# Score rounds in pairs in the middle steps, a reordered start, and shift and scale read back from DRAM

## The chip, the cores and the metric

The kernel runs on one core of a Trainium2 chip. The metric is the device time in microseconds (us) of one execution; the median of several runs is compared. A core has five engines that run side by side and meet at semaphores: PE (TensorE, matrix products), DVE (VectorE), ACT (ScalarE), POOL (GpSimd) and SP (SyncE, which here only issues transfers). PE writes to PSUM, which has eight banks; ACT and DVE read results from there.

## The reference

The input x is 8 sequences (B) of 256 tokens with 256 channels. Four blocks follow one another, each added to x. Cut to what matters:

```
x = x + attention_and_swiglu(x, cond)         # L0: conditioned norm, 16 heads of 16, softmax; then a gated MLP (1024)
x = x + modulated_attention(x, mask, cond)    # L1: 16 heads; out is normalised, then out * (1 + scale) + shift
x = x + quaternion_rotation(x)                # L2: reduces to a fixed 4x4 mixing of channel quarters
x = x + experts(x, cond)                      # L3: top 2 of 8 experts, three matrix products each

# L1's shift and scale, per sequence:
mod = silu(cond) @ Wc.T + bc                  # 8 x 512
shift, sc = split(mod);  xn = xn * rms_scale * (1 + sc) + shift
```

## The kernel before

**Order of work.** The program runs the sequences as a pipeline. A list `queue` holds the attention work of both layers in rounds: first layer "a0" of sequences 0, 1, 2, then in turn "a1" of sequence i and "a0" of sequence i+3. One call of `block()` (L1690) takes the next round: it computes scores for 8 heads (`c`) and half of the keys (`kc`), and if a pair of score rounds is complete, the values of that earlier pair. So each (sequence, layer) has four rounds, (c, kc) = (0,0), (0,1), (1,0), (1,1); values come behind the scores of the rounds with kc = 0, of the `c` before.

**A score round** (`Attention.scores`, L983) is eight matmul instructions on four groups of 32 rows of the array, into one PSUM tile of four banks (`ps_s`, one buffer), and one exponential over it on ACT (L990). **A values round** (L993) is 32 matmul instructions on four groups of 32 columns, into one bank (`ps_o`). All else on PE (projections, gates, transposes) shares three banks in turn (`ps_m`, through `bank()`), so a new tile waits until the third tile before it has been read.

**Steps.** `run(what, pieces, gaps, beside, starts)` (L1705) writes the order: for each letter "b" in `what` a round, then pieces of other work until the gap given for it is spent, `starts` before the pieces and `beside` after them. What a round's values complete (`then`: `after_first` with py, y; or `after_second` with py, o1) is done after three pieces. The middle steps are i = 2 to 6, each a `run("bbbbbbbb", others(i - 1), ...)` at L1901. `others` gives the pieces: gates pg, ph in four pairs with tanh (ACT), sg and hT (DVE), the product pd, then x2, its transpose pt_x, and the projections pk, pq, pv of the next rounds. `starts` and `beside` hold: `last` (the router of an earlier group, in steps 4 and 6, with four squarings on ACT at first), `n1` (norm of the sequence after next: squarings, then the divisor on DVE and two small transfers, then scaling), `n2` (the norm before the gates: squarings on ACT, divisor on DVE, two scalings on ACT, L900), `r1` and `rotated` (rotation on DVE).

In the whole program PE's instructions stand in the order of the text (`manual_schedule`), in the start DVE, ACT and POOL too, and DVE and ACT again from the middle steps on. SP's transfers go out in order, and each waits for its own data at the head of the queue.

**The start.** `first_norm(b)` yields three times: squarings, the divisor (`rsqrt`, eleven small DVE operations), the scaling. `first(b)` yields after the transposes (pt_n), pk, pq, pv. `prepare_condition` (L690) makes silu of the condition and `keyseen` from the mask; `prepare_router` (L748) prepares router constants; `set_up_condition` (L712) computes `mod` (8 x 512) on PE and writes it to DRAM as `mod_rows`, from where each sequence's row is later broadcast.

**Shift and scale on partitions.** `set_up_rotation` (L804) needs the same numbers the other way round, as `mc` (128 partitions x 4 x 8): it computes them a second time, in eight matmul instructions `pmc` (four products, L833) and two DVE operations. `scaled` reads `mc`, then come `phall`, `pshift`, `each`, and `pshg` (L862), one part after another as `second_step` (L1854) calls them.

Of the kernel before, what the change touches and what calls it, by code (L numbers as in the profile page):

```python
# [16 lines left out]
P = 128  # L17
# [17 lines left out]
WROW = B3O + D  # L35

SMALL = dict(condT=B, qrT=4, sgT=1, affb=4 * KC, rms=KC, wg=KC * E, ggw=E, wgb=E, ggb=E,
             wg4=4 * E, rms4=4, bcc=2 * KC, rsc=KC)

SL = 256  # L40

# [452 lines left out]
def block_kernel(ctx: ExitStack, tc: tile.TileContext, a: dict, out: bass.AP):  # L494
# [217 lines left out]
    def set_up_condition():  # L712

        pm = bank("pmod", (B, 2 * D))
        nc.tensor.matmul(pm, silu_c, wcT, start=True, stop=True)
        mod = wt("oT", [B, 2 * D], "mod_all")
        nc.vector.tensor_tensor(mod, pm, bc_b, ALU.add)
        nc.vector.scalar_tensor_tensor(mod[:, D:], mod[:, D:], 1.0, rs_b, ALU.add, ALU.mult)
        nc.gpsimd.dma_start(out=mod_rows, in_=mod)
        yield 0.4  # L720

    def set_up_slots():
# [81 lines left out]
    def set_up_rotation():  # L804
        prepare_rotation()

        nc.vector.tensor_tensor(
            wg4s, part["wg4"].rearrange("p (j e) -> p j e", e=E),
            part["rms4"].unsqueeze(2).to_broadcast([P, 4, E]), ALU.mult,
        )  # L810
        for h in range(2):
            r = slice(h * C, (h + 1) * C)
            nc.vector.tensor_copy(rmine[r], rotg[r].rearrange("p j (k h) -> p k h j", h=2)[:, :, h, :])
        turned = work.tile([P, KC, 4, E], F32, tag="raw", bufs=2, name="turned")
        nc.vector.tensor_tensor(
            turned, rmine.unsqueeze(3).to_broadcast([P, KC, 4, E]),
            wg4s.unsqueeze(1).to_broadcast([P, KC, 4, E]), ALU.mult,
        )
        nc.vector.tensor_reduce(gall, turned.rearrange("p k j e -> p k e j"), AX.X, ALU.add)
        nc.vector.tensor_copy(wv1[:, :, D:], gall)  # L820

        nc.sync.dma_start(out=coef_row, in_=rotg[0:C].rearrange("c j i -> c (j i)"))
        rows_in = wt("x4", [P, C, 4, 4], "coef_in", 1)
        nc.sync.dma_start(
            out=rows_in.rearrange("p c j i -> p (c j i)"),
            in_=coef_row.rearrange("c w -> (c w)").partition_broadcast(P),
        )
        yield
        nc.gpsimd.tensor_copy(coef, rows_in.rearrange("p c j i -> p i j c"))

        pm = bank("pmc", (P, 2 * KC, B))
        for k in range(2 * KC):
            nc.tensor.matmul(pm[:, k, :], wcT[:, k * P : (k + 1) * P], silu_c, start=True, stop=True)  # L833
        nc.vector.tensor_tensor(mc, pm, part["bcc"].unsqueeze(2).to_broadcast([P, 2 * KC, B]), ALU.add)
        nc.vector.scalar_tensor_tensor(
            mc[:, KC:], mc[:, KC:], 1.0, part["rsc"].unsqueeze(2).to_broadcast([P, KC, B]), ALU.add, ALU.mult
        )
        scaled = wt("mod", [P, KC, B, E], "scaled")
        nc.vector.tensor_tensor(
            scaled, mc[:, KC:].unsqueeze(3).to_broadcast([P, KC, B, E]),  # L840
            gall.unsqueeze(2).to_broadcast([P, KC, B, E]), ALU.mult,
        )
        yield
        ph = bank("phall", (P, KC, B * E))
        for c in range(KC):
            for k in range(KC):
                nc.tensor.matmul(
                    ph[:, c, :], wo1n[:, k, c * P : (c + 1) * P], scaled[:, k].rearrange("p b e -> p (b e)"),
                    start=k == 0, stop=k == KC - 1,
                )  # L850
        nc.vector.tensor_copy(hall.rearrange("p k b e -> p k (b e)"), ph)
        ps = bank("pshift", (B, E))
        for k in range(KC):
            nc.tensor.matmul(ps, mc[:, k, :], gall[:, k, :], start=k == 0, stop=k == KC - 1)
        each = work.tile([B, B, E], F32, tag="r_each", bufs=1, name="each")
        nc.vector.tensor_tensor(
            each, ps.unsqueeze(1).to_broadcast([B, B, E]),
            ident[0:B, 0:B].unsqueeze(2).to_broadcast([B, B, E]), ALU.mult,
        )
        yield  # L860
        pb = bank("pshg", (P, B * E))
        nc.tensor.matmul(pb, ones[0:B, :], each.rearrange("p b e -> p (b e)"), start=True, stop=True)  # L862
        nc.vector.tensor_copy(shg.rearrange("p b e -> p (b e)"), pb)
        yield
# [5 lines left out]
    def bank(name, shape=(P, 2, S)):  # L870
        return ps_m.tile(list(shape), F32, tag="m", name=name)
# [165 lines left out]
    def do(parts):  # L1037
        for _ in parts:
            pass
# [650 lines left out]
    def block():  # L1690
        layer, b, c, kc = queue.pop(0)
        second = layer == "a1"
        if (c, kc) == (0, 0):
            live[layer, b] = Attention(
                state[b].pop(f"qkv{int(second)}"), f"{layer}_{b}", (2 * b + second) * KC
            )
        live[layer, b].scores(c, kc)
        then = values()
        if second and (c, kc) == (KC - 1, NQ - 1):
            nc.vector.tensor_copy(wo1[:, :, D:], hall[:, :, b, :])  # L1700
        if kc == NQ - 1:
            pending.append((layer, b, c))
        return then

    def run(what, pieces, us=0.0, beside={}, rest=True, owed=None, hold=False, soon=3, late_=(), starts={}):  # L1705

        spent, due, held = 0.0, 0.0, None
        for t, kind in enumerate(what):
            then = block() if kind == "b" else values() if kind == "v" else None
            do_deferred()
            for g in starts.get(t, ()):
                next(g, None)
            if held:
                held()  # L1720
                spent += 1.9
            held = None
            then, owed = then or owed, None
            if t in late_:
                held, then = then, None
            gap = us if isinstance(us, float) else us[t]
            due = max(due + gap, spent + min(gap, 3.0))
            n = 0
            while spent < due or (then and n < soon):
                w = next(pieces, "end")  # L1730
                if w == "break":
                    due = spent
                if w in ("break", "end"):
                    break
                spent += 1.9 if w is None else w
                n += 1
                if then and n == soon:
                    then()
                    spent += 1.9
                    then = None  # L1740
            if then and hold:
                return then
            if then:
                then()
                spent += 1.9
            for g in beside.get(t, ()):
                next(g, None)
        if rest:
            for _ in pieces:
                pass  # L1750

    def chain(*gens):
        for g in gens:
            yield from g
# [52 lines left out]
    with tc.manual_schedule(engines=by_text):  # L1807
# [10 lines left out]
        next(g0)  # L1818
        keep_busy(2)
        scales()  # L1820
        n1 = first_norm(1)
        next(n1)
        next(n1)
        next(g0)
        next(g0)
        do(n1)
        do(g0)
        blank = set_up_slots()
        prepare_condition()
        cond_g = prepare_router()  # L1830
        finish_slots(*blank)
        def third(b):

# [8 lines left out]


        operands = first(1)
        run("b", chain(take(1, operands), set_up_condition(), set_up_router(cond_g)), 9.0, rest=False)
        run("b", take(1, operands), 9.0, {0: [once(prepare_quaternions)]}, rest=False)
        n1 = first_norm(2)
        run("b", iter(()), 0.0, {0: [n1]})
        run("b", operands, 9.0, {0: [at_once(n1)]}, rest=False)
# [4 lines left out]
        def second_step():  # L1854
            rotation = set_up_rotation()
            next(rotation)
            yield
            n1 = first_turned(3)
            next(n1)
            yield  # L1860
            n2 = in_parts(1, "n2")
            next(n1)
            next(n2)
            next(rotation)
            yield
            do(n1)
            next(n2)
            next(rotation)
            set_up_ones()
            yield  # L1870
            do(n2)
            yield from rotation

        set_up = second_step()
        gaps = [1.9, 5.0, 7.2, 7.2, 7.2, 7.2]
        run("bbbbbb", chain(operands, others(0)), gaps, {n: [set_up] for n in range(1, 6)}, soon=2)
    by_text = {mybir.EngineType.DVE, mybir.EngineType.Activation}
    text_order = ctx.enter_context(ExitStack())
    text_order.enter_context(tc.manual_schedule(engines=by_text))
# [1 line left out]
    for i in range(2, B - 1):  # L1881
# [14 lines left out]
        if i == B - 2:  # L1896
# [1 line left out]
            early = table("early", (NG - 2) * NTG, EARLY, ALU.is_ge)  # L1898
            beside[4].insert(0, early)
            beside[7].append(early)  # L1900
        run("bbbbbbbb", others(i - 1), gaps, beside, late_=() if i + 2 < B else (4,), starts=starts)  # L1901


    pieces = others(B - 2)
# [206 lines left out]
```

## Time and profile before

| | |
|---|---|
| median of 8 runs | 703.54 us (703.05 to 706.36) |
| profiled execution: its own time | 706.39 us |
| its span, first to last instruction | 704.6 us |
| granted TensorE clock, mean | 0.997 |
| PE busy | 691.1 us (98%) |
| DVE, ACT, POOL busy | 366.1 (52%), 255.4 (36%), 180.3 (26%) |

Stages of the span, from first score round to first score round:

| stage | us | PE busy | DVE busy | ACT busy |
|---|---|---|---|---|
| up to the first scores | 0 to 18.60 | 17.10 | 7.33 | 5.55 |
| start, sequences 0 to 2 | 18.60 to 95.30 | 75.59 | 41.91 | 36.77 |
| step 2 | 95.30 to 148.48 | 53.16 | 30.24 | 23.74 |
| step 3 | 148.48 to 201.65 | 53.15 | 32.03 | 23.94 |
| step 4 | 201.65 to 255.87 | 53.78 | 38.64 | 25.92 |
| step 5 | 255.87 to 309.03 | 53.14 | 31.87 | 23.93 |
| step 6 | 309.03 to 358.49 | 48.60 | 36.83 | 24.52 |
| end of the attention | 358.49 to 441.0 | 81.49 | 54.48 | 32.85 |
| experts | 441.0 to 704.6 | 255.13 | 92.73 | 58.16 |

All times are those of one profiled execution, counted from its first instruction. A timeline line gives the start, the length, the engine, the line of the program, the operation, what it writes and reads, and in brackets how long the engine was idle before it and what ended that. Matmul instructions overlap, so the distance from one start to the next says more than the length. "PEld" is PE's loading of weights beside the products.

### The profile page before, as it was taken

Reading aid. Unit: us, or ns where it says so; the run is one execution under the profiler, and the core shown is the slowest. Engines: PE = TensorE matmul, PEld = TensorE weight load, DVE = VectorE, ACT = ScalarE, POOL = GpSimd, SP = SyncE. Lnnn points to the kernel's source line nnn. Section 1 sums busy time; section 2 is a strip of 40 time slices with the busy share of each in tenths; the row PEclk is TensorE's granted clock in tenths of the full one; section 3 lists DMA queues with packets and bytes.
Section 4 is the critical chain, followed back from the end, with each engine's and each line's share of the span. In section 5 each row is a group of like instructions: output and inputs, shape, how many; then the busy total and the mean of one; then the engine's idle time right before and its main releaser. Section 6 shows DMA issues by size and latency. Waiting matters only on the chain.

```text
span 704.6 us, 11187 instructions
## 1 busy us (share of the span) xinstructions
PE 691.1 (98%) x4258; PEld 534.0 (76%) x4258; DVE 366.1 (52%) x1165; ACT 255.4 (36%) x411; POOL 180.3 (26%) x223
## 2 busy tenths in 40 slices
PE   9999999999999999999999999999999999999995
PEld 8557777667766766766666786688888998999894
DVE  3664436576478476477575686688321222222221
ACT  3663234344354345355434236322221222222120
POOL 5511401001000141000230016324374432342213
PEclk9999999999999999999999999999999999999998
DMA  9411101002022000020000050837585866576712
GB/s 304 146 32 45 39 1 38 1 16 39 5 71 39 0 18 8 1 75 1 2 16 1 16 203 10 308 127 218 145 289 157 236 240 193 170 266 191 253 26 29
DMA packets 28878, 70.01 MB, mean 99 GB/s; under 512 B 9032, under 2 KB 22224, under 8 KB 26384
## 3 DMA queue, kind: packets, MB, share of 16 engines
q1 hardware_dynamic: 20032, 57.70, 24.8%
q0 software_dynamic: 8496, 11.32, 7.4%
q8 instruction: 35, 0.57, 0.3%
q14 instruction: 27, 0.22, 0.1%
q10 hardware_dynamic: 288, 0.18, 0.1%
HBM read 59.67 MB, written 9.53 MB: 98 GB/s over the span
## 4 chain that ended last, share of the span: by engine, by line
PE 92%; DVE 5%; ACT 2%; issue 1%; POOL 0%; POOLq 0%; DVEq 0%; ACTq 0%
PE ph_a_rest L1528 10%; PE s_a L988 9%; PE pd L1141 8%; PE pg L1128 8%; PE ph_a_p L1528 7%; PE ph L1128 7%; PE o_a L1001 7%; PE ph_s_sure L1528 6%; PE pq_a L932 3%; PE pe_a_rest L1558 3%; PE pk_a L932 3%; PE pe_a_p L1558 3%; PE pv_a L954 2%; PE py L1024 2%; PE pe_s_sure L1558 2%; PE py L1174 2%
## 5 line engine op out<-in xcount | busy, mean ns | idle before, releaser
L990 ACT ACTIVATE pe_a<-s_a 128x2048 f32<-128x2048 f32 x64 | 120.1, 1876 | 100.3 <-PE s_a L988 100.2
L988 PE MATMUL s_a<-qz_a,kT_a 32*128 32x512 f32 x512 | 73.0, 639 | 2.4 <-DVE xg L1159 0.9
L1001 PE MATMUL o_a<-pe_a,va 128*32 128x256 f32 x1024 | 61.9, 382 | 0.0
L1128 PE MATMUL pg<-xT_n,gate_wT 128*128 128x256 f32 x256 | 61.8, 384 | 0.0
L1128 PE MATMUL ph<-xT_n,hid_wT 128*128 128x256 f32 x256 | 61.6, 383 | 0.0
L1001 PEld LDWEIGHTS o_a<-pe_a,va 128*32 128x32 f32 x1024 | 30.0, 109 | 39.9 <-issue 23.4
L1141 PE MATMUL pd<-out_wT,hT 128*128 128x256 f32 x256 | 59.7, 384 | 0.4 <-DVE hT L1136 0.4
L1141 PEld LDWEIGHTS pd<-out_wT,hT 128*128 128x128 f32 x256 | 47.4, 190 | 13.7 <-issue 4.0
L1128 PEld LDWEIGHTS ph<-xT_n,hid_wT 128*128 128x128 f32 x256 | 47.7, 190 | 13.3 <-DVE rq_v_n L619 2.3
L1128 PEld LDWEIGHTS pg<-xT_n,gate_wT 128*128 128x128 f32 x256 | 47.6, 190 | 12.0 <-issue 3.6
L1010 DVE STREAM_TRANSPOSE tu_a<-o_a 128x512 f32<-128x512 f32 x32 | 22.8, 712 | 52.3 <-PE o_a L1001 52.3
L1528 PE MATMUL ph_a_rest<-h_a_rest,w_a_rest 128*128 128x256 f32 x224 | 49.6, 379 | 0.0
L1528 PEld LDWEIGHTS ph_a_rest<-h_a_rest,w_a_rest 128*128 128x128 f32 x224 | 42.0, 190 | 5.4
L1101 POOL TENSOR_TENSOR xy<-y,x 128x512 f32<-128x512 f32 x8 | 10.2, 1270 | 139.2 <-DVE rq_v_r L619 55.0
L1539 DVE TENSOR_SCALAR h_a_rest<-ph_a_rest,w_a_rest 128x256 f32<-128x256 f32 x28 | 13.6, 484 | 57.3 <-PE ph_a_rest L1528 56.3
L1316 POOL DMA_INDIRECT slots<-rec,posi x32 | 31.8, 994 | 22.6 <-issue 7.3
L1134 DVE SCALAR_TENSOR_TENSOR sg<-th,pg 128x512 f32<-128x512 f32 x32 | 21.9, 685 | 28.3 <-ACT th L1132 28.3
L988 PEld LDWEIGHTS s_a<-qz_a,kT_a 32*128 32x128 f32 x512 | 20.0, 182 | 21.5 <-issue 13.4
L1528 PE MATMUL ph_a_p<-h_a_p,w_a_p 128*128 128x192 f32 (+2 forms) x224 | 36.0, 319 | 0.0
L1132 ACT ACTIVATE th<-pg 128x512 f32<-128x512 f32 x32 | 19.0, 594 | 46.4 <-PE pg L1128 46.4
L1537 ACT ACTIVATE h_a_rest<-ph_a_rest,w_a_rest 128x256 f32<-128x256 f32 x28 | 13.3, 473 | 60.7 <-DVE h_a_rest L1539 60.7
L1528 PEld LDWEIGHTS ph_a_p<-h_a_p,w_a_p 128*128 128x128 f32 x224 | 34.9, 191 | 0.1
(351 smaller groups left out, 1185.8 us busy)
## 6 DMA issues: line engine op xcount, KB each, us to landing
w_a_rest<-in_experts SPq DMA_DIRECT2D x7, 2180.0 KB, 9.5
w_a_p<-in_experts SPq DMA_DIRECT2D x7, 2180.0 KB, 9.1
w_s_sure<-in_experts SPq DMA_DIRECT2D x4, 2180.0 KB, 10.2
w_s_early<-in_experts SPq DMA_DIRECT2D x1, 2180.0 KB, 8.7
mod<-mod_rows SPq DMA_DIRECT2D x8, 256.0 KB, 3.3
tokens<-x SPq DMA_DIRECT2D x4, 512.0 KB, 3.8
out<-x SPq DMA_DIRECT2D x4, 512.0 KB, 4.9
x<-in_x SPq DMA_DIRECT2D x7, 256.0 KB, 2.8
```

Of the source, the lines that this page charges most:

```text
L932: nc.tensor.matmul(pp[:, c, :], w[:, k, c * P : (c + 1) * P], xT[:, k, :], start=k == 0, stop=k == KC - 1)
L988: nc.tensor.matmul(sc[:, j], kT[r, c, kc * P : (kc + 1) * P], qz[r, c], start=True, stop=True)
L990: nc.scalar.activation(pe, sc, AF.Exp)
L1001: nc.tensor.matmul(o[32 * i : 32 * i + 32, qd, :], va[:, kc, 8 * c + 4 * qd + i].rearrange("p a d -> p (a d)"), pe[:, 2 * qd + i // 2, i % ...
L1010: nc.vector.transpose(turned.rearrange("p q j a d -> p (q j a d)"), o.rearrange("p q s -> p (q s)"))
L1128: nc.tensor.matmul(ps[:, j, :], w[:, k, o : o + P], yT[:, k, :], start=k == 0, stop=k == KC - 1)
L1132: nc.scalar.activation(th, pg, AF.Tanh, scale=0.5)
L1134: nc.vector.scalar_tensor_tensor(sg, th, 1.0, pg, ALU.add, ALU.mult)
L1141: nc.tensor.matmul(pd[:, t, :], hT[:, c, t * P : (t + 1) * P], out_w[:, c, :], start=c == 0, stop=c == HID // P - 1)
L1316: sc = nc.gpsimd.indirect_dma_start(out=slots, out_offset=bass.IndirectOffsetOnAxis(ap=posi[:, t : t + 1], axis=0), in_=rec[:, t, :], in_o ...
L1528: nc.tensor.matmul(ph[:, c - c0, 0:many], w[:, o : o + P], src[:, k, 0:many], start=k == 0, stop=k == n_in - 1,)
L1558: nc.tensor.matmul(pos[q][0:p, q, :], h2[:, k, q * p : (q + 1) * p], w[:, o : o + D], start=k == 0, stop=k == MC - 1,)
```

## The change

Four edits.

- In the middle steps two score rounds stand next to each other: with `pairs=True` the even letters call `block()` twice, the odd ones none. The gaps, the pieces and what stands beside them stay.
- In the start the condition and router constants come ahead of the norm of sequence 1; that norm's divisor comes behind the first queries, its scaling behind the first score round; pt_n and pk of sequence 1 both come behind the second round.
- `mc` is read from `mod_rows` in DRAM, in four transfers on SP's queue with a transposing access pattern, in place of the four products and two DVE operations. Its two columns of constants leave the small input.
- The last part of the rotation constants (`pshg`) comes at the head of the sixth round of the second stage's run, ahead of the last part of n2.

```diff
-             wg4=4 * E, rms4=4, bcc=2 * KC, rsc=KC)
+             wg4=4 * E, rms4=4)
...
         nc.gpsimd.dma_start(out=mod_rows, in_=mod)
+        for j in range(2 * KC):
+            nc.sync.dma_start(out=mc[:, j, :], in_=mod_rows[:, j * P : (j + 1) * P].rearrange("b p -> p b"))
...
         nc.gpsimd.tensor_copy(coef, rows_in.rearrange("p c j i -> p i j c"))
-        pm = bank("pmc", (P, 2 * KC, B))
-        for k in range(2 * KC):
-            nc.tensor.matmul(pm[:, k, :], wcT[:, k * P : (k + 1) * P], silu_c, start=True, stop=True)
-        nc.vector.tensor_tensor(mc, pm, part["bcc"]..., ALU.add)
-        nc.vector.scalar_tensor_tensor(mc[:, KC:], mc[:, KC:], 1.0, part["rsc"]..., ALU.add, ALU.mult)
         scaled = wt("mod", [P, KC, B, E], "scaled")
...
-            then = block() if kind == "b" else values() if kind == "v" else None
+            then = None
+            if pairs:
+                if t % 2 == 0:
+                    then = block()
+                    block()
+            else:
+                then = block() if kind == "b" else values() if kind == "v" else None
...
         scales()
+        prepare_condition()
+        cond_g = prepare_router()
         n1 = first_norm(1)
         next(n1)
-        next(n1)
         next(g0)
         next(g0)
-        do(n1)
+        next(n1)
         do(g0)
         blank = set_up_slots()
-        prepare_condition()
-        cond_g = prepare_router()
         finish_slots(*blank)
...
-        run("b", chain(take(1, operands), set_up_condition(), set_up_router(cond_g)), 9.0, rest=False)
-        run("b", take(1, operands), 9.0, {0: [once(prepare_quaternions)]}, rest=False)
+        run("b", chain(set_up_condition(), set_up_router(cond_g)), 9.0, {0: [at_once(n1)]}, rest=False)
+        run("b", take(2, operands), 9.0, {0: [once(prepare_quaternions)]}, rest=False)
...
             set_up_ones()
             yield
+            next(rotation)
+            yield
             do(n2)
-            yield from rotation
...
-        run("bbbbbb", chain(operands, others(0)), gaps, {n: [set_up] for n in range(1, 6)}, soon=2)
+        run("bbbbbb", chain(operands, others(0)), gaps, {n: [set_up] for n in range(1, 6)}, soon=2, starts={5: [set_up]})
...
-        run("bbbbbbbb", others(i - 1), gaps, beside, late_=() if i + 2 < B else (4,), starts=starts)
+        run("bbbbbbbb", others(i - 1), gaps, beside, late_=() if i + 2 < B else (4,), starts=starts, pairs=True)
```

More of the change, by code (lines that the diff above doesn't have):

```diff
@@ L829, in set_up_rotation @@
         nc.gpsimd.tensor_copy(coef, rows_in.rearrange("p c j i -> p i j c"))
-        pm = bank("pmc", (P, 2 * KC, B))
-        for k in range(2 * KC):
-            nc.tensor.matmul(pm[:, k, :], wcT[:, k * P : (k + 1) * P], silu_c, start=True, stop=True)
[L834 to L837, printed above, removed]
         scaled = wt("mod", [P, KC, B, E], "scaled")
@@ L1703, in block, with run @@
         return then
-    def run(what, pieces, us=0.0, beside={}, rest=True, owed=None, hold=False, soon=3, late_=(), starts={}):
+    def run(what, pieces, us=0.0, beside={}, rest=True, owed=None, hold=False, soon=3, late_=(), starts={}, pairs=False):
         spent, due, held = 0.0, 0.0, None
         for t, kind in enumerate(what):
-            then = block() if kind == "b" else values() if kind == "v" else None
+            then = None
[5 more added lines that the diff above has]
+                then = block() if kind == "b" else values() if kind == "v" else None
             do_deferred()
@@ L2083 @@
         rms4=np.tile(v["L3_cond_rms_w"].reshape(4, C).T, (2, 1)),
-        bcc=chunks(v["L1_cond_bc"]),
-        rsc=chunks(v["L1_cond_rms_scale"]),
     )
```

## The prediction

> **What bounds the kernel now.** I read the page's chain first (PE carries 92% of it), then PE's waits, then PE's timeline through one middle step, then ACT and DVE beside the places where the change moves work. In PE's waits (us in total, times, longest) nothing is left to win: six waits in 704.6 us, 4.5 us together.
>
> ```profile
> ...
> PE s_a L988 <- DVE xg L1159: 0.9, 1, 0.9
> ...
> PE pd L1141 <- DVE hT L1136: 0.4, 1, 0.4
> PE s_a L988 <- ACT pe_a L990: 0.2, 1, 0.2
> ```
>
> PE's timeline in step i = 3 (start us, us, what): a score round (s_a), a values round (o_a), and the "other" pieces pg, ph, pd between them.
>
> ```profile
> 153.24 1.89 PE L1128 MATMUL ph<-xT_n,hid_wT 128*128 128x256 f32 x8
> 154.97 1.89 PE L1128 MATMUL pg<-xT_n,gate_wT 128*128 128x256 f32 x8
> 156.70 1.89 PE L1024 MATMUL py<-L_WoT_turned,oT_a 128*128 128x256 f32 x8
> 158.52 1.14 PE L988 MATMUL s_a<-qz_a,kT_a 32*128 32x512 f32 x8
> 159.59 1.99 PE L1128 MATMUL ph<-xT_n,hid_wT 128*128 128x256 f32 x8
> 161.42 1.89 PE L1128 MATMUL pg<-xT_n,gate_wT 128*128 128x256 f32 x8
> ...
> 166.04 1.93 PE L1001 MATMUL o_a<-pe_a,va 128*32 128x256 f32 x32
> 167.90 1.99 PE L1128 MATMUL pg<-xT_n,gate_wT 128*128 128x256 f32 x8
> ```
>
> From start to start a piece of eight matmuls takes 1.73 (153.24 to 154.97), 1.82 when a score round follows (156.70 to 158.52) and 1.83 when one went before (159.59 to 161.42). A score round takes 1.07 (158.52 to 159.59), values after scores 1.86 (166.04 to 167.90). So each visit from the full array to these rounds, which split it into four groups, costs 0.09 + 0.10 = 0.19 beside its own work. The exponential of a score round (128x2048 on ACT) takes 1.88, and the scores have one buffer: the next round may start only after it.
>
> **The pairs themselves: +0.4 (0 to +1.4).** A pair before is scores, values, pieces, scores: 1.07 + 1.86 + 0.10 + 0.09 + 1.07 + 0.10 = 4.29 without the pieces. After, it is scores, values, scores, and the second scores wait for the first's exponential. The trace has such a triple, after the middle steps, and three pairs bound by the exponential at the start:
>
> ```profile
> 434.37 1.14 PE L988 MATMUL s_a<-qz_a,kT_a 32*128 32x512 f32 x8
> 435.44 1.93 PE L1001 MATMUL o_a<-pe_a,va 128*32 128x256 f32 x32
> 437.57 1.14 PE L988 MATMUL s_a<-qz_a,kT_a 32*128 32x512 f32 x8 [0.19 <-ACT pe_a L990]
> ```
>
> Scores to scores is 3.20 here, 3.13 at the start (18.60 to 21.73). A pair is then 3.13 to 3.20 + 1.07 + 0.10 = 4.30 to 4.37: the saved visit (0.19) is given to a wait of 0.20 to 0.27. Twenty pairs (five steps of four): 0.2 to 1.6 worse; I take 0.4. ACT does not start the first exponential late: before each even round its last work is a copy or nothing, and it sits idle 0.5 us or more.
>
> [...]
>
> **What the odd score rounds covered.** Their 1.26 us (1.07 + 0.19) lay between a piece and the piece that needs its result; now they lie ahead.
>
> *Steps 2, 3, 5: +1.6 (0 to +1.6).* With the first score round of t=2 at 0: second at 3.13, its exponential on ACT 4.33 to 6.21, and ACT runs in text order, so the two scalings of n2 (L900, 0.90; called by `starts[2]`) and then the tanh of the last gate (0.60) come after it: tanh ends 7.65, DVE's sg 7.68 to 8.37, hT 8.43 to 9.12. PE does pg from 4.20 (3.13 + 1.07), ph from 6.03 (+1.83), the first half of pd 7.76 (+1.73) to 8.62, and its second half needs that hT: wait 0.54. Before, a score round stood ahead of pd and the exponential came 3.1 earlier (tanh at 169.93, no wait at 172.62). Three steps.
>
> *Step 4: +2.4 (+1.2 to +2.6).* Here `last` and n1 put six squarings on ACT behind the exponential, and DVE is full from y to the last hT:
>
> ```profile
> ...
> 207.79 0.58 ACT L1132 ACTIVATE th<-pg 128x512 f32<-128x512 f32 x1
> ...
> 211.79 0.69 DVE L1100 TENSOR_TENSOR y<-py,x 128x512 f32<-128x512 f32 x1 [0.41 <-PE py L1024]
> ...
> 228.32 0.69 DVE L1136 TENSOR_TENSOR hT<-sg,ph 128x512 f32<-128x512 f32 x1
> ...
> 229.06 2.86 PE L1141 MATMUL pd<-out_wT,hT 128*128 128x256 f32 x12 [0.42 <-DVE hT L1136]
> ```
>
> The exponential of that step's first round began at 202.91; from there to the tanh is 4.88. From the step's first round at 0 the second exponential starts at 4.33, tanh 9.21, sg ends 10.51; py takes the third bank round, so that of pg: it starts at 10.55, not 9.49. Then y starts at 10.55 + 1.93 = 12.48, before at 211.79 - 201.65 = 10.14. DVE needs 229.01 - 211.79 = 17.2 from there, without a gap: hT at 29.7, pd's second half 29.75, before 229.06 - 201.65 = 27.41. Difference 2.3, and 0.1 for the wo copy (L1700), now ahead of that hT. Without the bank wait it would be 1.25.
>
> *Step 6: +1.5 (+0.1 to +1.6).* Same, shorter: four squarings, y 1.3 later, and pd's bank waits for the hT before it. That hT ended 13.7 after y (319.18, 332.86), so now at 11.5 + 13.7 = 25.2, where PE stands from 24.5; the scores of t=4 start at 26.2, before at 335.10 - 309.03 = 26.07: 0.1. Then the odd round moves from behind pd (344.44) ahead of it, so x2 is 1.4 later, and from x2 (344.03) to qz and the scores at 358.49 the chain is DVE's (place, o1, divisor, rotate), as PE's 0.9 wait there says.
>
> Late in each step (t=4 to 7) I find the covers thinner, but left: qz of the next block is ready 0.2 ahead of its scores.
>
> **The start: +1.2 (+1.0 to +1.3).** PE's first rounds:
>
> ```profile
> 18.60 1.14 PE L988 MATMUL s_a<-qz_a,kT_a 32*128 32x512 f32 x8
> 19.67 0.66 PE L888 MATMUL pt_n<-ident,xs_n 128*128 128x128 f32 x4
> ...
> 21.73 1.14 PE L988 MATMUL s_a<-qz_a,kT_a 32*128 32x512 f32 x8
> ...
> 24.87 1.14 PE L988 MATMUL s_a<-qz_a,kT_a 32*128 32x512 f32 x8
> ```
>
> Rounds come every 3.13, and pt_n fits into the first gap. Moving queries ahead of the divisor wins nothing: DVE sat idle 1.62 before qz_a (16.98). But the scaling of block 1 now follows the first exponential on ACT (21.7 to 22.6), pt_n goes behind the second round (22.8), where pk stands now (22.81 to 24.8), its xT on DVE 23.4 to 24.4 (0.64 after pt_n, then two of 0.5), pk ends at 26.0, and the third round starts at 26.1. The next ones hang on it by 3.13 and by pieces without gaps, so 1.2 stays.
>
> Put ahead on DVE: nine small operations of 0.15 to 0.2 us, in the idle time from 12.3 to 16.98. One waits for the mask: queued behind it are qz and the first scores. Its landing isn't shown. A zero transfer behind it on POOL's queue landed 6.8 after its issue at 9.62, so by 16.4; at worst the scores start 2.4 late (landed at 18.3, where keyseen ran). I take 0. The divisor of block 1 (2.15 of DVE) now stands between qz and `blank`, so POOL's transfers from 20.76 on (slots, second layer's weights, mod_rows) go out some 0.5 later; their first reader is PE at 78. Cost 0.
>
> **Shift and scale from DRAM: +0.15 (-0.9 to +0.9).** Gone: eight matmuls (pmc, 67.53 to 68.51: 0.98 of PE) and two DVE operations (0.36), and six columns of a load. PE gains only 0.3 of that: the hT that pd waits for ends at 74.16, and DVE (divisor until 70.98, then scaled, transposes, hT) shortens by 0.36 alone. The small matmul pshg moves from 86.02 to just behind the round at 79.57 and needs `each` (DVE, 81.48 to 81.68, behind rb's landing at 78.2): PE waits from 80.3 to 81.7 for 1.4, pd, pk, pq behind it. Given back: 0.68 + 0.2 at pv (87.71), whose bank was then the one of qz. Sum -0.3 + 1.4 - 0.9 = +0.15.
>
> Added: four transfers on SP's queue, 1024 runs of 4 bytes each. They wait for mod_rows, as `mod` did (issued 29.47). Behind them on SP: `mod` (needed at 88), x (41.49), xr (41.97), coef_row (50.53). The reader is `scaled` on DVE at 71. Per packet the first 60 us show 0.033 us of a transfer engine (the ACT queue, 288 packets, 1.0% of 16 engines) to 0.136 (software queue, 816, 11.6%): 4096 packets on 16 engines take 8.5 to 35, so they land at 41 to 67. Cost 0; if not, all of DVE stands from 71 on.
>
> [...]
>
> **Sum.** 0.4 + 1.6 + 2.4 + 1.5 + 1.2 + 0.15 = 7.25. The profiled execution took 706.39 (span 704.6 and 1.8 around it), 2.85 above the median of the runs, 703.54. I make the sum a difference of spans (704.6 to 711.9) and put it on the median: 710.8. The low ends add up to +1.5, the high ends to +11.8 with the mask.
>
> **Rivals.** *Only the saved visits count* (faster): the exponential is over when the values are, and what follows stays covered. 20 x 0.19 + 0.98 = 4.8 less: 698.8. It decides if scores to scores can be 2.93 or less; all of the rows show 3.13 or more. 5%. *The uncovered tails find slack* (no change): only pairs, start and rotation are left, +1.75: 705.3. Against it stands that PE arrives first in each of the three sums, by 0.5 at least. 9%. *The mask is late*: +9.65, 713.2, 9%. *The element transfers are late*: bounded only by the 3.1 us of a 128-packet transfer (rstd_rows), 32 times that is 99 us, 57 too late: 715 to 768, 5%. That the pairs don't form can't be: each step has eight rounds and begins with kc=0.
>
> **Numbers.** My case: 72%, 710.8. A measurement here tells 0.3%, 2.1 us, from no change. Faster 0.05; same 0.09; slower 0.86. Range 705.0 (the low ends and the second rival) to 714.5 (the mask, or most of the high ends).
>
> **What would show it.** PE waits for ACT's pe_a some 20 times, 0.2 to 0.27 each; pd waits for hT 0.5 in steps 2, 3, 5. Steps (first round to first round) before 53.2, 53.2, 54.2, 53.2, 49.5 become 53.8, 53.8, 56.6, 53.8, 51.0; 18.60 to 95.31 becomes 78.1; the third round starts at 26.1. Steps at 52.4, or no waits for pe_a, would prove me wrong; so would a wait of DVE on mc or on the mask.

## The result and the profile after

The changed kernel took 710.58 us (median of 11 runs, 708.92 to 716.0), the kernel before 703.1 (32 runs) beside it: a ratio of 1.011, with a 95% interval of 1.0089 to 1.0131. It is 7.5 us slower; the forecast was 710.8. The profiled execution took 715.44 (span 713.7), that of before 706.39 (704.6), so the spans differ by 9.1, 1.6 more than the medians; where that comes from is shown below.

The stages, from first score round to first score round, in the two profiles:

| stage | before | after | difference | forecast |
|---|---|---|---|---|
| up to the first scores | 18.60 | 18.53 | -0.07 | 0 |
| start | 76.71 | 81.08 | +4.37 | +1.35 |
| step 2 | 53.17 | 53.10 | -0.07 | +0.6 |
| step 3 | 53.17 | 53.11 | -0.06 | +0.6 |
| step 4 | 54.22 | 56.84 | +2.62 | +2.4 |
| step 5 | 53.16 | 53.10 | -0.06 | +0.6 |
| step 6 | 49.46 | 51.94 | +2.48 | +1.5 |
| all later | 346.1 | 346.0 | -0.1 | 0 |

PE's waits after (us in total, times, longest):

```profile
PE pd L1136 <- DVE hT L1131: 2.6, 2, 1.8
PE s_a L983 <- ACT pe_a L985: 2.1, 3, 1.2
PE pshg L857 <- DVE each L851: 2.1, 1, 2.1
...
PE py L1019 <- DVE sg L1129: 1.0, 1, 1.0
PE pk_a L927 <- DVE xT_n L919: 0.6, 1, 0.6
```

Before, pd waited 0.4 in all and no row named pshg, py or pk. The 20 small waits for pe_a that I had announced are not in this list: in the pair at 152.71 the values' weight loads end at 155.24 and their products at 155.71, and the wait stands with the loads (0.62 there; the profile after counts 16.5 us in all in which the weight loads of s_a had waited for pe_a). It is seen in the distances. PE's timeline after, at the places that the forecast worked out (start, length, what, in brackets the idle time before it):

```profile
22.74 0.66 PE L883 MATMUL pt_n<-ident,xs_n 128*128 128x128 f32 x4
24.04 2.01 PE L927 MATMUL pk_a<-xT_n,L_WkT 128*128 128x256 f32 x8 [0.64 <-DVE xT_n L919]
25.98 1.14 PE L983 MATMUL s_a<-qz_a,kT_a 32*128 32x512 f32 x8
...
82.94 0.68 PE L857 MATMUL pshg<-each,ones 8*128 8x64 f32 x2 [2.10 <-DVE each L851]
83.55 3.78 PE L1136 MATMUL pd<-out_wT,hT 128*128 128x256 f32 x8
87.12 2.98 PE L927 MATMUL pk_a<-xT_n,L_WkT 128*128 128x256 f32 x8
...
123.86 5.34 PE L1136 MATMUL pd<-out_wT,hT 128*128 128x256 f32 x24
...
152.71 1.14 PE L983 MATMUL s_a<-qz_a,kT_a 32*128 32x512 f32 x8
...
155.85 1.14 PE L983 MATMUL s_a<-qz_a,kT_a 32*128 32x512 f32 x8
...
216.46 1.99 PE L1019 MATMUL py<-L_WoT_turned,oT_a 128*128 128x256 f32 x8 [0.98 <-DVE sg L1129]
...
235.85 2.86 PE L1136 MATMUL pd<-out_wT,hT 128*128 128x256 f32 x12 [1.77 <-DVE hT L1131]
...
341.21 1.99 PE L1136 MATMUL pd<-out_wT,hT 128*128 128x256 f32 x8 [0.85 <-DVE hT L1131]
...
360.74 1.14 PE L983 MATMUL s_a<-qz_a,kT_a 32*128 32x512 f32 x8 [1.23 <-ACT pe_a L985]
```

In the order of the lines: the third round comes at 25.98 behind pt_n, DVE and pk in one row; pshg waits 2.10, and pd and pk behind it take 3.57 and 2.83 from start to start, where 1.8 is usual; in step 2 pd runs through its 24 instructions unbroken; in step 3 a pair is 3.14 from scores to scores; steps 4 and 6 hold the new waits. In step 4 the first of them can be followed on ACT:

```profile
210.22 1.88 ACT L985 ACTIVATE pe_a<-s_a 128x2048 f32<-128x2048 f32 x1 [1.32 <-PE s_a L983]
...
215.10 1.06 ACT L1127 ACTIVATE th<-pg 128x512 f32<-128x512 f32 x2
```

The second exponential stands ahead of six squarings and the tanh, so the tanh starts 9.28 after the step's first round (205.82); the forecast had 9.21.

### The profile page after: what moved, and what is told of

Read it like the earlier page. It is cut to its first block, busy times and chain, and to the rows that moved or that the text cites. A ratio compares the mean times of both kernels' runs of the same rounds, so it can differ in the third digit from the quotient of the medians.

```text
span 713.7 us, 11170 instructions
## 1 busy us (share of the span) xinstructions
PE 691.1 (97%) x4250; PEld 536.0 (75%) x4250; DVE 365.8 (51%) x1163; ACT 256.3 (36%) x411; POOL 180.9 (25%) x223
## 4 chain that ended last, share of the span: by engine, by line
PE 83%; DVE 8%; ACT 6%; DMA 1%; issue 1%; POOL 0%; POOLq 0%; DVEq 0%; ACTq 0%
PE ph_a_rest L1523 10%; PE s_a L983 9%; PE ph_a_p L1523 7%; PE pd L1136 7%; PE pg L1123 7%; PE ph L1123 6%; PE ph_s_sure L1523 6%; ACT pe_a L985 6%; PE pk_a L927 4%; PE pq_a L927 3%; PE pe_a_rest L1553 3%; PE pe_a_p L1553 3%; PE o_a L996 2%; PE py L1019 2%; PE pv_a L949 2%; PE pe_s_sure L1553 2%
## 5 line engine op out<-in xcount | busy, mean ns | idle before, releaser
L1136 PE MATMUL pd<-out_wT,hT 128*128 128x256 f32 x256 | 61.2, 391 | 2.6 <-DVE hT L1131 2.6
L983 PEld LDWEIGHTS s_a<-qz_a,kT_a 32*128 32x128 f32 x512 | 20.0, 182 | 29.3 <-ACT pe_a L985 16.5
L941 DVE TENSOR_SCALAR qz_a<-pq_a,par 128x512 f32<-128x512 f32 x32 | 22.5, 746 | 26.0 <-PE pq_a L927 26.0
```

Source lines behind the costliest of these rows:

```text
L941: nc.vector.tensor_scalar(qz[:, :, j, :], pq, par[:, j : j + 1], None, ALU.mult)
L983: nc.tensor.matmul(sc[:, j], kT[r, c, kc * P : (kc + 1) * P], qz[r, c], start=True, stop=True)
L1136: nc.tensor.matmul(pd[:, t, :], hT[:, c, t * P : (t + 1) * P], out_w[:, c, :], start=c == 0, stop=c == HID // P - 1)
```

## The experiments

Theory A: a pair by itself costs nothing (the saved visit goes to the wait for the exponential), and the losses are covers taken away in steps 4 and 6, the start's row, and pshg's wait with the low granted clock behind it (the share of full speed at which TensorE was let run). The rivals are named with each run. To read the times: nine of the twelve runs fell on a chip on which the kernel before takes 728 to 731 us instead of 703, where in the profiles taken there PE waits up to 7 us late in steps 4 and 6 and again after step 6 (I did not find out why). I call it the slower chip, and read rounds there up to the seventh of a step, which repeat on both chips to 0.05 us. The kernel before was run there in two sets, with medians of 730.87 and 728.18, and each ratio is to one of them, so the stages say more than the ratios.

**The changed kernel again** (control of its three neighbours).

> The changed kernel once more, as the measure for the three beside it. Theory A: each stage as in its first profile (first scores to step 2 81.1, steps 53.1, 53.1, 56.8, 53.1, 51.9), if the wait at pshg (2.0 or more) again takes the granted clock to 0.50. If that low clock hangs on chance, this stage is 78.2 and the rest the same.

Measured: ratio 1.0179 (1.0141 to 1.0216) on the slower chip; first scores to step 2 80.73; steps 2 and 3 53.10; in step 4 the third, fifth and seventh rounds at 17.74, 32.79, 48.50 (first chip: 17.74, 32.82, 48.53). The stages repeat. pshg waited 1.62 here, less than the 2.0 that I had made the condition, and the low clock came all the same, for 6.8 us.

**Rounds apart again.** `run(..., starts=starts, pairs=True)` becomes

```diff
-        run("bbbbbbbb", others(i - 1), gaps, beside, ..., starts=starts, pairs=True)
+        run("bbbbbbbb", others(i - 1), gaps, beside, ..., starts=starts)
```

> The changed kernel with the score rounds of the middle steps apart again; the start, mc from DRAM and pshg stay changed. Theory A (pairs cost nothing by themselves, but uncover ACT's and DVE's work in steps 4 and 6): steps 2, 3 and 5 stay at 53.1 each to 0.1, step 4 goes from 56.8 back to 54.2, step 6 from 51.9 to 49.5; 5.0 us faster than the changed kernel, about 705.5. Rival B (each pair is bound by the exponential and costs in every step, as the +0.4 and +1.6 of the forecast had it): steps 2, 3 and 5 fall as well, by 0.5 each, 703.9. Rival C (most of the loss lies in the start): under 2 us faster.

Measured: ratio 1.0049 (1.0019 to 1.008). Steps 2 and 3 53.17. Step 4's third, fifth and seventh rounds at 16.48, 30.21, 45.83, step 6's fifth and seventh at 26.07, 38.89: each within 0.01 of the kernel before. So the pairs cause all of the loss in steps 4 and 6 and none in steps 2 and 3: B falls. The ends of steps 4 and 6, and so the 5.0 in full, can't be read on this chip; by the seventh rounds it is 2.7 + 1.85. The rest is read on the other chip, from the kernel with pairs in steps 2, 3 and 5 only (below): there steps 4 and 6 take 54.22 and 49.45, as before.

**Only two pairs taken apart.** The first pair of step 4 and that of step 6:

```diff
-                if t % 2 == 0:
+            if t in pairs:            # (2, 4, 6) in steps 4 and 6, else (0, 2, 4, 6)
                 then = block()
                 block()
+            elif t - 1 not in pairs:
...
```

> The changed kernel, but the first pair of step 4 and the first pair of step 6 are taken apart (two of the twenty pairs). Theory A (the losses of these steps come from the second exponential ahead of the first squarings and tanh, which makes sg and so py, y and the last hT late): in step 4 the third round comes 16.5 after the first (17.74 as changed), the fifth 30.2 (32.8), in step 6 the fifth 26.1 (27.4); 2.6 + 1.3 = 3.9 us faster than the changed kernel, 4 us with luck in the end of step 6. Rival B (every pair of these steps costs something, by the exponential or by thinner covers of the later rounds): under half of that, 2 us or less.

Measured: ratio 1.0098 (1.0064 to 1.0131), against 1.0179 for the control. Step 4: third round 16.49, fifth 30.28, seventh 45.99. Step 6: fifth 26.07, seventh 39.44, where rounds apart give 38.89. Two pairs of twenty carry 2.5 + 1.3 us. Nearly all that is left is in step 6: the later pairs cost 0.55 up to the seventh round, and its last pair is 4.23 from scores to scores instead of 3.14 (the 1.23 wait at 360.74 in the first profile, where on ACT two squarings and x2T stand ahead of the exponential).

**A shorter exponential.**

```diff
-            nc.scalar.activation(pe, sc, AF.Exp)
+            nc.scalar.activation(pe[:, 0:3], sc[:, 0:3], AF.Exp)
```

> The changed kernel with the exponential over three of a round's four banks (128x1536 instead of 128x2048, some 1.4 us instead of 1.88); the values read the third bank's result in place of the fourth's, so a quarter of the attention weights is not computed. Theory A (in a pair the second round waits for the first's exponential, and that wait of 0.2 takes back the saved visit): the second round of a pair starts 2.93 after the first and takes 1.07 as ever, its exponential is over earlier too, and steps 2, 3 and 5 take 52.3 in place of 53.1. Rival B (scores, values, scores take 3.13 on PE by itself, or a step's length is set elsewhere): 3.13 and 53.1 stay.

Measured on the chip where before takes 703: steps 2, 3 and 5 take 52.29 each. PE's timeline of its step 3:

```profile
149.48 1.14 PE L983 MATMUL s_a<-qz_a,kT_a 32*128 32x512 f32 x8
...
152.42 1.14 PE L983 MATMUL s_a<-qz_a,kT_a 32*128 32x512 f32 x8
```

Scores to scores is 2.94, and a step is 0.88 shorter than with rounds apart, 0.22 a pair. In the kernel before PE is busy for 53.15 of a step's 53.17, so the shorter exponential had no other wait to take away. The visits are worth what I had read (0.19), and the exponential takes them back: this is shown now. The time of this kernel (709.01) still has the other losses.

**Two half exponentials**, meant to get that gain with the whole computation (start and pshg as before, mc from DRAM, pairs in steps 2, 3, 5 and in half of step 4):

```diff
-            sc = ps_s.tile([P, 4, 2, S], F32, tag="s", ...)
+            sc = [ps_s.tile([P, 2, 2, S], F32, tag=f"s{h}", ...) for h in range(2)]
...
-            nc.scalar.activation(pe, sc, AF.Exp)
+            for h in range(2):
+                nc.scalar.activation(pe[:, 2 * h : 2 * h + 2], sc[h], AF.Exp)
```

> A version meant to beat both: start and pshg as before, mc from DRAM, pairs in all of steps 2, 3, 5 and in the second half of step 4 only, and the scores of a round in two tiles of two banks with an exponential of 128x1024 for each, so that the second round of a pair may start when the first half is read. Theory A (the saved visit of 0.19 went to the wait for the exponential): the second round starts 2.93 to 3.0 after the first, steps 2, 3 and 5 take 52.3 to 52.6, and the kernel is 0.75 + 3 x 0.7 + 0.3 = 3 us faster than before. Rival B (the values in between, not the exponential, set the 3.13, or the two halves cost ACT 0.2 more a round and it gets late elsewhere): steps stay at 53.1 or grow; 0.7 faster at best, and slower than before if ACT becomes late.

Measured: ratio 1.0013 (0.9989 to 1.0038), steps 2 and 3 53.16 and 53.15. Its step 3:

```profile
147.54 1.14 PE L983 MATMUL s_a<-qz_a,kT_a 32*128 32x512 f32 x8
...
150.47 1.36 PE L983 MATMUL s_a<-qz_a,kT_a 32*128 32x512 f32 x8
151.76 1.99 PE L1124 MATMUL pg<-xT_n,gate_wT 128*128 128x256 f32 x8
```

The second round starts at 2.93 as A had it, but takes 1.29 instead of 1.07. The two half exponentials are over at 3.11 after the first scores (148.71 + 1.94), no sooner than the whole one, so the second half of the round, which needs the second tile, starts no sooner either. The pair ends at 4.22 as ever. My expectation overlooked that; the idea gains nothing.

**pshg back at the end of the second stage.**

```diff
-            next(rotation)
-            yield
             do(n2)
+            next(rotation)
...
-        run("bbbbbb", ..., soon=2, starts={5: [set_up]})
+        run("bbbbbb", ..., soon=2)
```

> The changed kernel with the product pshg back at the end of the second stage; all else stays changed. Theory A (pshg's 2.1 us wait for DVE stops PE, and the granted clock falls to 0.50 after it): the wait and the slow products behind it go (2.1 + 3.1), 0.9 of wait at pv comes back; first scores to step 2 falls from 81.1 to about 77.0, the clock stays at 0.97 or more in that stretch, and the run is 4 us faster, about 706.5. Rival B (the clock would fall there anyway, or the four small transfers cost the 3 us): only 1.2 us faster, 709.4, and the low clock stays.

Measured: ratio 1.0059 (1.0037 to 1.0081). First scores to step 2 is 77.08, granted clock 1.00 from 72 to 92: as theory A had it.

**Products in place of the wait.**

```diff
-        pb = bank("pshg", (P, B * E))
+        both = bank("pshg", (P, P))
+        for _ in range(12):
+            nc.tensor.matmul(both, ident, ident, start=True, stop=True)
+        pb = both[:, 0 : B * E]
```

> The changed kernel with twelve products of the identity (128x128, about 0.15 us each, 1.8 together) ahead of pshg in its own bank, so that PE works instead of waiting for DVE's each; the result doesn't use them. Theory A (the idle time of 2 us takes the granted clock to 0.50 for some 6 us after it): pshg still starts at the same time or 0.2 later, but pd, pk behind it take 1.83 each again: first scores to step 2 falls from 81.1 to 78.2 to 78.4, 2.8 us faster. Rival B (pd is slow there for another reason, as a busy memory or the transfers at 82): 81.1 to 81.3.

Measured: ratio 1.0139 (1.0104 to 1.0174), first scores to step 2 80.29. Its timeline:

```profile
78.80 2.94 PE L858 MATMUL pshg<-ident 128*128 128x128 f32 x24 [1.54 <-DVE hall L846]
81.67 0.43 PE L860 MATMUL pshg<-each,ones 8*128 8x64 f32 x2
82.03 1.99 PE L1139 MATMUL pd<-out_wT,hT 128*128 128x256 f32 x8
83.86 1.89 PE L930 MATMUL pk_a<-xT_n,L_WkT 128*128 128x256 f32 x8
```

pd is back at 1.83 (82.03 to 83.86), with a clock of 1.00 in all of these windows: B falls, the clock made pd and pk slow. That the products kept the clock up is not shown: their own wait of 1.54 was followed by no low clock, and the changed kernel too has a profile without one (the third, below). The stage did not become 78.3, because the products took 2.87 in all, 0.24 each, not 0.15, and had to wait 1.54 for their bank: pshg came 2.3 later.

**The start's order undone** (divisor of sequence 1 ahead of the queries, constants behind, pt_n and pk on two sides of the second round, as in the diff's removed lines).

> The changed kernel with the order of the start as before (divisor of sequence 1 ahead of the first queries, pt_n and pk of sequence 1 on both sides of the second round, constants behind). Theory A (the new order puts pt_n, its scaling on DVE and pk in one row behind the second round): the third round comes 6.27 after the first, not 7.45, and what follows keeps that: 1.2 us faster, 709.4. Rival B (the 1.2 is absorbed later, where PE waits for DVE at pshg): third round 1.2 earlier, but the wait at pshg grows by 1.2, and the time stays at 710.6.

Measured: ratio 1.0077 (1.0052 to 1.0103). The third round comes 6.28 after the first, and the twelfth 59.99 after it, where the changed kernel has 61.17: 1.18 is kept, A. The stage takes 78.16, 2.9 less than in the first profile of the changed kernel: 1.18 of that is the start's, and the rest goes with the shorter low clock, 3.4 us, behind pshg's wait of 1.77.

**mc from DRAM alone**, twice. The kernel before with pmc's eight products and two DVE operations out, and the four transfers in.

> The kernel before with one edit: mc comes from DRAM in four transfers of 4-byte runs, and pmc's eight products and two DVE operations are gone; rounds, start and pshg as before. Theory A (the transfers land long before DVE reads them and PE has nothing to wait for in that place): PE gains pmc's 0.98 in full, 1.0 us faster than before, 702.1. As the forecast had it (pd waits for hT there anyway): 0.3 us faster. Rival B (the transfers delay x, xr or coef_row on SP's queue and so block 3, or the clock falls in that stretch): 1 to 4 us slower.

> The kernel before with mc from DRAM alone, a second time, to narrow the interval. Theory A: 0.75 to 1.0 us faster than before, a ratio of 0.9987; first scores to step 2 again 76.0. Rival B (the four transfers or the later clock take the gain back): a ratio of 1.000 or more.

Measured: ratios 0.9985 (0.9961 to 1.0009) and 0.9989 (0.9969 to 1.0009). Up to the twelfth round the gain is 0.98 (59.99 and 59.98 against 60.97); first scores to step 2 takes 75.97 and 76.32 against 76.71. So pmc's time is won in full and 0.2 to 0.6 of it is given back, in the second run to a wait of 0.36 of pk for DVE. Both intervals reach past 1: that this is faster than before is likely, and not shown by the times.

**What is left without the costly places**: that, and pairs in steps 2, 3 and 5 only.

> What is left of the change when its costly places are undone: start and pshg as before, mc from DRAM, pairs in steps 2, 3 and 5 alone. Theory A (pairs cost nothing where ACT and DVE have slack): steps 2, 3, 5 at 53.1, steps 4 and 6 as before up to their last round (51.1 and 43.8), first scores to step 2 76.0; 0.95 us faster than before, a ratio of 0.9987. Rival B (pairs cost in each step): a ratio over 1.001.

Measured: ratio 0.9999 (0.9978 to 1.0021); stages as A says (75.91; 53.10, 53.10, 53.16; steps 4 and 6 54.22 and 49.45). B falls. Added up, its stages from first scores to the end of step 6 are 0.95 shorter than before (338.94 against 339.89); the times can't tell it from before.

**The changed kernel a third time.**

> The changed kernel a third time, one look, for the spread of its times (709, 710.5 and 715.5). Theory A (two places where the low clock may last longer or shorter): the first scores begin either at 14.6 to 15.1 or at 18.2 to 18.6, by how long the clock stays low from 5 us on, and first scores to step 2 takes 78.2 to 81.1, by how long it is 0.50 behind pshg; a run of 710.5 is one with 14.9 and about 79.4. Steps 2 to 6 are 53.1, 53.1, 56.8, 53.1, 51.9 in every case. Rival B (the spread comes from elsewhere, the transfers or the experts): first scores at 18.5 and 81.1 at another total time.

Measured (on the slower chip, 738.96): first scores at 18.10, steps 2 and 3 53.1, and 78.21 from first scores to step 2, with pshg's wait at its longest:

```profile
82.73 0.43 PE L857 MATMUL pshg<-each,ones 8*128 8x64 f32 x2 [2.34 <-DVE each L851]
83.10 1.99 PE L1136 MATMUL pd<-out_wT,hT 128*128 128x256 f32 x8
84.93 1.89 PE L927 MATMUL pk_a<-xT_n,L_WkT 128*128 128x256 f32 x8
```

No low clock followed. So without a low clock the move of pshg costs 78.21 - 77.08 = 1.13 (one profile of each), and the clock adds nothing, or 1.2 (79.39 in the kernel with two pairs apart), or 2.9 (81.08). Which of these a run of 710.5 has was not seen directly. The mean granted clocks on record for the changed kernel's runs fit 1.2: 0.997 at 708.9 and 709.0, 0.994 or 0.995 in the seven runs from 709.8 to 710.8, and 0.993 in the four from 715.2 to 716.0; a stretch of 3.4 us at half the clock is 0.0024 of 709 us.

## Why the prediction was right, and where its steps were not

The direction, the size and the places held; the sum (7.25 against 7.5) is better than its terms, since errors of both signs cancel.

- **Pairs (+0.4).** Right in mechanism, shown by the shorter exponential; the size is -0.02 a pair. Twenty saved visits of 0.19 alone, as the first rival counts them, would be 3.8 us faster; that agrees with the 0.22 a pair that appear once the exponential is short, and the wait decides.
- **Steps 2, 3, 5 (+1.6): wrong, -0.2.** The failed step is "the first half of pd 7.76 (+1.73) to 8.62". One piece of pd is eight instructions and takes 1.73, not 0.86 (24 take 5.28, 123.86 to 129.14), and it reads four of eight column blocks; the last hT feeds the seventh, some 2.6 after pd begins. In step 2 that hT ended at 125.11, needed at 126.45. Slack of 1.3 stood where I put a wait of 0.54; pd's only two waits after are in steps 4 and 6.
- **Step 4 (+2.4): right, +2.62.** py waited 0.98 for sg (forecast 1.06), and pd 1.77 for hT where it had waited 0.42.
- **Step 6 (+1.5): half.** I let PE arrive at 24.5 and lose 0.1 up to t=4, with the same short pd; pd waited 0.85 and the fifth round came at 27.37, not 26.2. By the kernel with two pairs apart the first pair cost 1.30 where I had 0.1, which leaves 1.18 for the rest, where I had 1.4, and part of that in another place: the wait of 1.23 at the last pair, behind squarings on ACT, is one that I had declared covered ("thinner, but left"). I had written that ACT sits idle ahead of each even round's exponential. At the last pair of step 6 the trace before says otherwise: the round began at 347.92, and its exponential waited 0.5 for ACT and began behind two squarings and x2T, with no idle time ahead of it:

```profile
349.49 1.88 ACT L990 ACTIVATE pe_a<-s_a 128x2048 f32<-128x2048 f32 x1
```

- **The start (+1.2): right, +1.18.** The mask was no matter: keyseen ran at 12.22, with 3.6 us of idle time left before qz.
- **Shift, scale and pshg (+0.15).** mc gave 0.8 (0.74, 0.39 and 0.80 in three kernels) instead of 0.3. It is the same mis-sized pd: before, pd began at 73.28 and the hT that ended at 74.16 was not read until some 2.6 later, so it did not hold PE. The move of pshg cost 1.13; I had 1.4 of wait less 0.9. The wait was 2.10, since PE won pmc's 0.98 in full and not 0.3: with the start 1.18 later, the twelfth round came at 79.70 beside 79.57, while rb's landing, behind which `each` stands, came 1.20 later (79.42 beside 78.22). The clock behind it, 0 to 2.9, was no term of the sum; if the median run has 1.2 of it and the profiled one 2.9, that is the 1.6 by which the spans differ more than the medians.
- **The transfers (0): right.** The landings, by the profile after:

```profile
mc<-mod_rows SPq DMA_DIRECT2D x4, 4.0 KB, 2.9
```

Issued from 29.59 to 32.20, 2.8 to 3.5 us each to landing, so over before 36; the reader came at 72.10. Even my lower bound (41) was too late. It was worked out from 33 ns of engine time a packet, read off ACT's queue. In the window of 28 to 34.2 us, ahead of the load of `mod` that stands behind them, the queue's 3906 packets took 34.1% of 16 engines, 33.8 us of engine time or 8.7 ns a packet: for 4096 packets on 16 engines that is 2.2 us, where the lower bound had 8.5.

Added without the clock: -0.2 + 2.62 + 2.48 + 1.18 - 0.8 + 1.13 = 6.4, or 709.5; with 1.2 for the clock 710.7 (with 0.4 for mc, the least that was seen, 0.4 more). The low ends of the forecast's terms add up to +1.4, not +1.5, so its range should begin at 704.9. The rival of the uncovered tails in slack was right for steps 2, 3 and 5 and wrong where ACT and DVE have `last`, n1 and r1 to do.

## What to carry to other kernels

Pulling work of one kind together saves a switch, but what lay between was cover: look, at each place, for the work of the other engines that is now late (here a second exponential ahead of six squarings cost 2.5 us in one step and nothing in its neighbours). When you place a wait inside a piece, count which instruction of the piece reads the late operand, and how long the pieces before it take, from a row with its count of instructions. A wait of TensorE can have a second price, a lower clock behind it: here waits of 1.6 to 2.3 us at one instruction cost nothing, 1.2 or 2.9 us more, from profile to profile.

## What was not expected of the hardware

The granted clock behind pshg's wait, in windows of the first profile after (columns: window, its length, PE, PEld, DVE, ACT, POOL busy with their instructions, PEclk, DMA share, GB/s):

```profile
82.00:84.00 2.00, 1.06 (x3) 0.95 (x4) 1.03 (x6) 0.79 (x1) 1.90 (x3) 0.62 0.53 153
84.00:86.00 2.00, 2.00 (x6) 1.55 (x6) 0.00 (x0) 0.00 (x0) 2.00 (x2) 0.50 0.00 0
86.00:88.00 2.00, 2.00 (x7) 1.55 (x6) 0.56 (x1) 0.00 (x0) 1.91 (x2) 0.50 0.00 0
88.00:90.00 2.00, 2.00 (x8) 1.65 (x7) 0.13 (x1) 0.00 (x0) 2.00 (x3) 0.67 0.02 4
```

If the clock is 0.50 or 1.00, these means make 1.52 + 4 + 1.32 = 6.84 us of low clock; the clock records in the trace itself, which these windows average, have 0.50 from 82.50 on for 6.83 us. Computed so, the seven profiles with this wait give 6.8 (waits of 2.10, 1.97 and 1.6), 3.4 (1.82, 1.77 and 1.69) and none (2.34). The length of the wait does not order them; the low time came in steps of 3.4, and what sets that step was not shown. A wait of 1.6 was enough here. It was not enough everywhere: behind pd's wait of 1.77 in step 4 of the first profile after the clock stayed at 1.00.

The first scores began at 14.6 to 15.1 in some profiles and at 18.1 to 18.6 in others, for the same kernel too; the 16 instructions of paff take 3.58 in the latter and 2.17 in one of the former (the kernel without the costly places), while the view gives a granted clock of 1.00 in both. But the traces hold no clock record ahead of 5.3 to 6.4 us in the profiles with the early start, and none ahead of 13.4 to 14.5 us in those with the late one (14.36 in that of before, 14.23 in the first one after), so the 1.00 shown ahead of that is not a measurement. That PE's clock was low until then fits paff's times and is not shown directly. Runs of the kernel before lie at about 703 and 706, which fits: its profiled run of 706.39 has 18.60, that of mc alone at 705.84 has 18.46, and that without the costly places at 701.57 has 14.91. The runs without a profile were not tied to it. For the changed kernel 709.0 + 2.9 for the clock + 3.5 for a late start makes 715.4, the time of its first profile, which has both.
